# Indirect gathers issued behind other engines' steps: behind tanh in an attention, behind expert units in a tail

## The chip, the core, the metric

The kernel runs on one core of a Trainium2 chip. A time is the device time of one execution in microseconds (us); the time of the kernel is the median of ten. The engines are called PE (matrix multiply), ACT (activations), DVE (vector), POOL (GpSimd) and SP (which only issues DMAs here). Each engine works through its own list of instructions in order; engines wait for each other on semaphores.

## What is computed

The input is 4 images of 32 x 96 positions with 256 channels: 12288 tokens in 4 batches of 3072. Layer 0 is a group norm and two state space scans, along the 96 segments and along the 32 variables. Layer 1 first has an additive attention in each batch, and then a mixture of experts whose gates come from a graph attention over 1048576 edges. Only the parts named below matter here.

```python
# attention: q = t @ Wt, k = t @ Wx, t = layer norm of the tokens
h = tanh(q[:, :, None, :] + k[:, None, :, :] + bh)        # 3072 x 3072 x 32 in each batch
a = softmax(h @ Wa); t = t + a @ t_normed
# graph attention over edges src -> dst; indices past the last token are clamped or dropped
e = leaky_relu(a_src[src] + a_dst[dst])
ee = exp(e - e_max[dst]); alpha = ee / segment_sum(ee, dst)[dst]
agg = segment_sum((x @ W_gat)[src] * alpha, dst)          # 4 heads x 4 features for each token
w = softmax(top2(mean over heads(layer_norm(agg))))       # gates of 4 experts
out = sum over experts e of w_e * (gelu(x @ W1[e] + b1[e]) @ W2[e] + b2[e])
```

## The kernel before, in words

**Stages.** Layer 0 runs first, with the attention of the batches that are done beside it. The last attention, of batch 3, runs after layer 0 has ended; beside it run a sort of the edges on DVE, a count of the edges that end at the last token (class `Edges`), and expert units whose gates are not yet needed. Then comes `tail`: the rest of the expert units, the graph attention, and the sums weighted by gates. The order of instructions on PE, ACT, DVE and POOL is the order in which the program is written; no scheduler changes it, but for the few instructions after the tail.

**The last attention.** Each of its 768 slots has one tanh on ACT (`th`, L814, 128 x 3072, three buffers), 16 matmuls that read it two slots later (`pe`, L787), and small steps of softmax, transposes and products. `steps()` runs between them: in each slot it adds some DVE work of the sort, some PE work of the count (`pc`, L1216) and of early expert units. When the sort and the count are done, it makes a pool `late2` in the memory that they have left, loads the experts' weights there, and places the tile `gd` there. From then on each slot issues two indirect gathers on POOL:

```python
for _ in range(2 if columns else 0):
    ed.gather(*columns.pop(0))
```

One gather fetches, for each of 128 partitions, one row of 4 floats from the table `tab_a` into a column of `gd` (L1037); the rows' numbers are in `di`, which the sort made. There are 4 parts of 108 columns, one part for each batch of destinations. Parts 0 to 2 (324 gathers) can be fetched in the last attention; part 3 (108 gathers) needs that attention's result.

**The tail.** PE, ACT and DVE work through steps `t`. An expert unit (a block of 512 tokens and one expert) takes three steps: four times a product `ph` (L1608) with its gelu (L1690) into the tile `h1` (two buffers), and one unit later two outputs `po` (L1616) whose sum with a bias DVE writes to the tile `ko` (L1680, two buffers), from where SP stores it (`kept`). 37 units are left for the tail, which is 111 steps. Beside them 36 groups of 12 edge columns run: group `m` has its scores (L1331 to L1335, L1258, L1259) at step `G0 + PART * m // 2`, with `G0, PART = 10, 5`, and in the steps after it three spreads (DVE: one-hots `ol`, `oh` at L1350, `rh` at L1354) and three placements (PE: `pa`, L1364, 24 matmul records for a group). Each quarter of the groups closes with `finish` (L1374 to L1433), which makes the gates of six blocks. A block's final sum then reads its four stored outputs (`all`) and its tokens (`y`), 16 additions on DVE (L1693), and stores the result; these sums stand four steps apart, from the step after the gates are ready on.

**The gathers of the tail.** Group `j` needs 12 gathers from `tab_s` into `gs` (L1314, four buffers), and while part 3 of `gd` is missing each group's batch brings 4 gathers of it along: 16 for a group up to `j = 26`, 12 after that, 540 in all. The first group's gathers are issued ahead of the step loop, ahead of a POOL reduction `topa` (L1280); those of group `j` are placed ten steps ahead of its scores. On POOL nothing else stands between them; a gather waits only for the buffer that it writes and for the eighth gather before it.

Of the kernel before, what the change touches and what calls it, by code (L numbers as in the profile page):

```python
# [26 lines left out]
P = 128  # L27
# [32 lines left out]
G1, K1 = 8, 4  # L60
GP, GG = 12, 4
EDGE_US = 2.4
G0, PART = 10, 5
KO_BUFS = 2
SLOT_US, PRODUCT_US = 1.2, 0.11
EU, EG = 32, 2
# [572 lines left out]
class Attention:  # L639
# [4 lines left out]
    def __init__(self, ctx, tc, ident, a, x1, x2, xn2T, tab_s, tab_a):  # L644
        self.nc = nc = tc.nc
        self.ident, self.x1, self.x2, self.xn2T = ident, x1, x2, xn2T
        self.tab_s, self.tab_a = tab_s, tab_a
        pool = lambda name, bufs, **k: ctx.enter_context(
            tc.tile_pool(name=name, bufs=bufs, side="right", **k))
        const = self.const = pool("atc", 1)  # L650
        self.rows, self.th, self.wk = pool("atr", 2), pool("atb", TH_BUFS), pool("atw", 1)
        self.ps_e = pool("ate", PE_BUFS, space=PSUM)
        self.ps_v = pool("atv", PV_BUFS, space=PSUM)

        def load(name, shape, ap):
            t = const.tile(shape, F32, tag=name, name=name)
            nc.sync.dma_start(t, ap)
            return t

        self.wt = load("wt_rep", [P, KC, P], a["wt_rep"].rearrange("(k p) m -> p k m", p=P))  # L660
        self.wx = load("wx_rep", [P, KC, P], a["wx_rep"].rearrange("(k p) m -> p k m", p=P))
        self.bh = load("bh_rep", [P, 1], a["bh_rep"])
        self.wa = load("wa_blk", [P, P // (4 * R_ATT), QU], a["wa_blk"])
        self.ba = load("ba_rep", [P, 1], a["ba_rep"])
        self.wg = load("wg", [P, KC, HF], a["W_gat"].rearrange("(k p) f -> p k f", p=P))
        self.asr = load("as_rep", [P, HF], a["as_rep"])
        self.adr = load("ad_rep", [P, HF], a["ad_rep"])
        self.eps = const.tile([P, 1], F32, tag="eps1", name="eps1")
        nc.vector.memset(self.eps, 1e-5)

        self.sel = const.tile([P, QU], F32, tag="sel", name="sel")
        nc.vector.tensor_tensor(self.sel, ident[:, :QU], ident[:, QU:2 * QU], ALU.add)
        for q in range(2, P // QU):
            nc.vector.tensor_tensor(self.sel, self.sel, ident[:, q * QU:(q + 1) * QU], ALU.add)
        self.state = [{} for _ in range(B)]

        self.krep, self.qsel = ([const.tile([P, n], F32, tag=f"{k}{i}", name=f"{k}{i}") for i in range(2)]
                                for k, n in (("krep", TOK), ("qsel", TOK // R_ATT)))
        self.extra, self.entry, self.col, self.asked, self.normed = 0.0, 0, 0, 0, 0

        self.later = []

    def psum(self, name):
        return self.ps_v.tile([P, JB], F32, tag="pv", name=name)
# [90 lines left out]
    def units(self, side):  # L775
# [24 lines left out]
        while i < B * PER + LAG or todo or self.later:  # L800
# [10 lines left out]
            if b < B:  # L811
                s = self.state[b]
                th = self.th.tile([P, TOK], F32, tag="th", name="th")
                nc.scalar.activation(th, s["krep"], AF.Tanh, bias=s["qsel"][:, col:col + 1])  # L814
                behind.append(th)
            yield
            late, self.later = self.later, []
            for f in late:
# [192 lines left out]
class Edges:  # L1011
# [3 lines left out]

    def __init__(self, ctx, tc, a):
        self.nc, self.tc, self.a, self.todo = tc.nc, tc, a, []
        keep = ctx.enter_context(tc.tile_pool(name="el", bufs=1))  # L1020
        new = lambda name, shape, dt=F32: keep.tile(shape, dt, tag=name, name=name)
        self.cnt = new("cnt", [P, NH])
        self.lost = new("lost", [P, 1])
        self.si, self.di = new("si", [P, 4, CQ], I32), new("di", [P, 4, CQ], I32)
        self.lane, self.tile = new("lane", [P, 4, CQ]), new("tile", [P, 4, CQ])
        self.lanes, self.tiles = new("lanes", [P, P]), new("tiles", [P, NH])
        self.nc.sync.dma_start(self.lanes, a["lanes"])

    def places(self, pool, tab_a):

        self.gd = pool.tile([P, 4, CQ, HEADS], F32, tag="gd", name="gd")
        self.tab_a, self.have = tab_a, set()

    def gather(self, q, c):
        if (q, c) not in self.have:
# [57 lines left out]
    def sort(self):  # L1093
# [4 lines left out]
        with ExitStack() as ctx:  # L1098
# [73 lines left out]
            v.tensor_scalar(hi, flat(x3), 7, None, ALU.logical_shift_right)  # L1172
            v.tensor_copy(flat(self.lane), lo)
            v.tensor_copy(flat(self.tile), hi)
            yield 1.5


# [11 lines left out]
            v.tensor_copy(l4, self.lanes.unsqueeze(2).to_broadcast([P, P, K1]))  # L1189
            v.tensor_copy(t4, self.tiles.unsqueeze(2).to_broadcast([P, NH, K1]))  # L1190
            yield 1.0
            p = ctx.enter_context(tc.tile_pool(name="eo", bufs=3))
            ps = ctx.enter_context(tc.tile_pool(name="ep", bufs=1, space=PSUM))
            pc = ps.tile([P, NH], F32, tag="pc", name="pc")
            starts = [q * W2 + g for q in range(4) for g in range(0, C1, G1)]

            def one_hots(c0):
                hot = []
                for name, table, of, n in (("ol", l4, lane, P), ("oh", t4, tile, NH)):
                    t = p.tile([P, G1 // K1, n, K1], BF16, tag=name, name=name)  # L1200
                    which = of[:, c0:c0 + G1].rearrange("p (g k) -> p g k", k=K1)
                    v.tensor_tensor(t, table.unsqueeze(1).to_broadcast([P, G1 // K1, n, K1]),
                                    which.unsqueeze(2).to_broadcast([P, G1 // K1, n, K1]),
                                    ALU.is_equal)
                    hot.append(t)
                return hot

            ahead = one_hots(starts[0])
            yield G1 * (P + NH) / 1800
            for i in range(len(starts)):  # L1210
                hot, ahead = ahead, one_hots(starts[i + 1]) if i + 1 < len(starts) else None

                def products(i=i, hot=hot):
                    for u in range(G1):
                        g, k = divmod(u, K1)
                        nc.tensor.matmul(pc, hot[0][:, g, :, k], hot[1][:, g, :, k],  # L1216
                                         start=(i == 0 and u == 0),
                                         stop=(i == len(starts) - 1 and u == G1 - 1))

                self.todo.append(products)  # L1220
                yield G1 * (P + NH) / 1800
# [6 lines left out]
class Graph:  # L1228
# [4 lines left out]
    def __init__(self, ctx, tc, a, ed, tab_s, tab_a, gates):  # L1233
# [5 lines left out]
        self.bg, self.lg, self.lb = (self.load(a, k, HF) for k in ("bg_rep", "lg_rep", "lb_rep"))  # L1239
        self.eps = self.new("eps2", [P, 1])  # L1240
        self.nc.vector.memset(self.eps, 1e-5)
        self.got, self.v, self.pa = {}, {}, {}

    def new(self, name, shape):
        return self.const.tile(shape, F32, tag=name, name=name)
# [59 lines left out]
        nc.vector.tensor_tensor(wl, wl, ed.cnt.unsqueeze(2).to_broadcast([P, NH, ROW]), ALU.mult)  # L1305
        nc.vector.tensor_tensor(acc, acc, wl, ALU.add)

    def gather(self, j):
        nc, ed = self.nc, self.ed
        gs = self.wk.tile([P, GP, ROW], F32, tag="gs", name="gs", bufs=4)  # L1310
        q, c0 = divmod(j * GP, CQ)
        rows = self.tab_s.rearrange("p n f -> (p n) f")
        for u in range(GP):
            nc.gpsimd.indirect_dma_start(  # L1314
                out=gs[:, u, :], out_offset=None, in_=rows,
                in_offset=bass.IndirectOffsetOnAxis(ap=ed.si[:, q, c0 + u:c0 + u + 1], axis=0))
            ed.gather(q, c0 + u)

        for c in range(4 * j, min(4 * j + 4, CQ)):
            ed.gather(3, c)  # L1320
        self.got[j] = gs

    def scores(self, j):
        nc = self.nc
        gs = self.got.pop(j)
        q, c0 = divmod(j * GP, CQ)
        gd = self.ed.gd[:, q, c0:c0 + GP, :]
        e = self.wk.tile([P, GP, HEADS], F32, tag="e", name="e")
# [377 lines left out]
def tail(tc, a, ed, ex, w, tab_s, tab_a, gates):  # L1706


    with ExitStack() as ctx:
# [11 lines left out]
            at(2 * n, lambda: next(own, None))  # L1721
        hot, ready = {}, {}
        PQ = CQ // GP
        for m in range(4 * PQ):
            j = m
            t = G0 + PART * m // 2
            if m < 1:
                gr.gather(j)
            else:
                at(max(0, t - 10), lambda j=j: gr.gather(j))  # L1730
            at(t, lambda j=j: gr.scores(j))
            for g in range(GP // GG):
                at(t + 1 + g, lambda j=j, g=g: hot.update({(j, g): gr.spread(j, g)}))
                at(t + 2 + g, lambda j=j, g=g: gr.place(j, g, *hot.pop((j, g))))
# [36 lines left out]
        for t in range(max(3 * len(units) + 3, end)):  # L1771
# [3 lines left out]
            if n < len(units):  # L1775
# [9 lines left out]
                    ex.fetch(units[n + 1][0])  # L1785
                for f in ((0, 1), (2,), (3,))[part]:
                    ex.gelu(i, e, f, hs[n])
            if n and n - 1 < len(units) and part:
                i, e = units[n - 1]
                ex.outputs(i, e, hs[n - 1], 2 * (part - 1), to[n - 1], i not in kept)  # L1790
                if part == 2:
                    if i in kept:
                        ex.keep(i, e, to[n - 1])
# [100 lines left out]
def whole(tc, a, dram, out):  # L1894
# [11 lines left out]
    with ExitStack() as ctx:  # L1906
        actx, lctx, ectx = ExitStack(), ExitStack(), ExitStack()
        with tc.manual_schedule(engines={E.PE, E.Activation, E.DVE, E.Pool}):
# [10 lines left out]
            def steps():  # L1919
# [7 lines left out]
                lctx.close()  # L1927
                keep = ctx.enter_context(tc.tile_pool(name="late", bufs=1))
                late["gates"] = keep.tile([P, NH, NEXP], F32, tag="gates", name="gates")
                ed = late["ed"] = Edges(ctx, tc, a)  # L1930
                ex = late["ex"] = Experts(ectx, tc, x2, xn2T, late["gates"], out, dram, l0.beside)
                lists, units, columns = ed.sort(), None, []

                us_v = us_t = 0.0
                while True:
                    us_v = min(us_v, 0.0) + EDGE_US
                    while lists and us_v > 0 and len(ed.todo) < 2:
                        us = next(lists, None)
                        if us is None:
                            lists = None  # L1940
                            pool = ectx.enter_context(tc.tile_pool(name="late2", bufs=1))
                            late["w"] = Experts.weights(pool, nc, a)
                            ed.places(pool, tab_a)
                            columns = [(q, c) for q in range(B - 1) for c in range(CQ)]
                        else:
                            us_v -= us
                    yield
# [8 lines left out]
                             if (i, e) not in ex.done], a, att.krep[B % 2])  # L1956
                    while units and us_t > 0:
                        us_t -= next(units, 1.0) or 0.0
                    for _ in range(2 if columns else 0):
                        ed.gather(*columns.pop(0))  # L1960
                    yield

# [99 lines left out]
```

## Time and profile before

| what | value |
|---|---|
| median of 10 runs | 15298.12 us (15287.41 to 15314.91) |
| the profiled execution | 15310.4 us, of which the profile's span 15308.6 us |
| busy share of the span | PE 77%, ACT 80%, DVE 72%, POOL 57% |
| last attention, first tanh to last | 11773 to 14251 us |
| gathers `gd` of parts 0 to 2 | first at 13647.7 us, last at 14136.3 us |
| first product of the tail's units, first gather of the tail | 14317.0 us, 14294.2 us |
| last gather of the tail, last output of a unit | 15119.9 us, 15249.8 us |
| last addition of a final sum ends | 15303.0 us |

Read it in this way: the profile's times count from the start of its span; they are of one execution, which was 12.3 us longer than the median. A busy share is an average over stages with different limits, so what follows reads the stages by themselves: the last attention and the tail.

### The profile page before, as it was taken

What the parts mean: (1) busy time and instruction counts of PE and PEld (TensorE: products, weight loads), DVE (VectorE), ACT (ScalarE), POOL (GpSimd) and SP (SyncE); (2) the same over time, 40 slices, a digit from 0 to 9 for tenths busy, and PEclk for the clock granted to TensorE, in tenths of its full rate; (3) what the DMA queues carried; (4) which work ended last, traced back from release to release, by engine and by line L of the source; (5) the groups of instructions that cost most, each with busy time, mean ns of one, the idle gap of its engine ahead of it and who ended that gap; (6) DMA issues with size and microseconds to landing.
All of it is one profiled execution on the core that took longest, in us unless ns stands there. A gap on an engine that the chain in (4) does not pass through costs nothing. (4 is left out here: it accounts for less than half of the span.)

```text
span 15308.6 us, 224326 instructions
## 1 busy us (share of the span) xinstructions
PE 11744.2 (77%) x86496; PEld 5136.8 (34%) x86496; DVE 10995.4 (72%) x15895; ACT 12175.2 (80%) x9333; POOL 8747.2 (57%) x6402
## 2 busy tenths in 40 slices
PE   5666665777777778888887777788876778888997
PEld 2222232222222233333333333333332334433554
DVE  7888888778777887777777877577768863331367
ACT  3444434999999979999999899999997889999422
POOL 4555556777777767767777677477650000026584
PEclk8888886888888878899999889989988989999998
DMA  5666665445544444454444444355541000011235
GB/s 190 204 204 202 199 202 167 149 147 154 153 151 151 157 155 147 150 154 151 151 151 153 152 149 152 109 151 151 151 136 39 20 16 12 9 30 24 64 92 147
DMA packets 1209114, 2007.86 MB, mean 131 GB/s; under 512 B 412385, under 2 KB 655713, under 8 KB 1204961
## 3 DMA queue, kind: packets, MB, share of 16 engines
q1 hardware_dynamic: 1180384, 1988.07, 41.6%
q0 software_dynamic: 27648, 5.36, 0.9%
q8 instruction: 680, 11.14, 0.3%
q14 instruction: 402, 3.29, 0.1%
HBM read 1875.19 MB, written 117.83 MB: 130 GB/s over the span
## 5 line engine op out<-in xcount | busy, mean ns | idle before, releaser
L814 ACT ACTIVATE th<-krep,qsel 128x3072 f32<-128x3072 f32 x3072 | 8669.5, 2847 | 411.2 <-PE pe L787 393.5
L787 PE MATMUL pe<-th,wa_blk 128*32 128x384 f32 x49152 | 5058.8, 540 | 1661.6 <-ACT pr L875 1437.3
L408 POOL TENSOR_TENSOR h<-h,bC 128x768 f32<-128x768 f32 x2048 | 3753.9, 1833 | 3019.8 <-DVE h L401 2638.9
L401 DVE TENSOR_TENSOR_SCAN h<-dA,dB 128x384 f32<-128x384 f32 x4096 | 3686.1, 941 | 1037.5 <-ACT dA L384 717.4
L787 PEld LDWEIGHTS pe<-th,wa_blk 128*32 128x32 f32 x49152 | 1453.4, 116 | 4245.7 <-issue 1990.0
L392 DVE TENSOR_TENSOR dB<-bB,dtu 128x768 f32<-128x768 f32 x2048 | 1941.7, 948 | 126.5 <-DMA bB<-bc 94.0
L384 ACT ACTIVATE dA<-dt,t_A 128x380 f32<-128x380 f32 x2048 | 1126.5, 570 | 900.5 <-DVE h L401 895.9
L384 ACT ACTIVATE dA<-dt,d_A 128x372 f32<-128x372 f32 x2048 | 1102.7, 561 | 607.3 <-DVE h L401 602.7
L427 PE MATMUL py<-h,ident 128*128 128x384 f32 x2176 | 981.2, 582 | 687.9 <-POOL h L408 686.8
L415 POOL TENSOR_TENSOR h<-h 128x768 f32<-128x768 f32 x752 | 1418.9, 1887 | 53.7
L950 POOL TENSOR_SCALAR sf<-sel,f 128x32 f32<-128x32 f32 x384 | 148.8, 412 | 2252.0 <-ACT f L946 2252.0
L891 PE MATMUL pv<-xn,pT 128*32 128x257 f32 x18432 | 1113.3, 390 | 141.7 <-DVE pT L884 140.7
L884 DVE COPY pT<-ptw 128x512 f32<-128x512 f32 (+1 forms) x768 | 418.8, 545 | 713.3 <-PE ptw L882 713.1
L427 PEld LDWEIGHTS py<-h,ident 128*128 128x128 f32 x2176 | 431.4, 216 | 1246.7 <-POOL h L408 1023.6
L891 PEld LDWEIGHTS pv<-xn,pT 128*32 128x32 f32 x18432 | 582.9, 112 | 727.5 <-DVE pT L884 269.6
L417 POOL TENSOR_TENSOR y<-y,h 128x384 f32<-128x384 f32 x752 | 782.6, 1041 | 59.0
L416 POOL TENSOR_TENSOR h<-h 128x384 f32<-128x384 f32 x752 | 782.0, 1040 | 59.0
L1314 POOL DMA_INDIRECT gs<-tab_s,si x432 | 533.8, 1236 | 155.5 <-issue 147.3
L893 DVE COPY pvs<-pv 128x257 f32<-128x257 f32 x384 | 160.5, 418 | 591.6 <-PE pv L891 590.2
L882 PE MATMUL ptw<-ident,pr 128*128 128x128 f32 x2304 | 476.6, 324 | 117.0 <-DVE pT L884 46.4
L868 DVE TENSOR_REDUCE nb<-pe 128x1 f32<-128x768 f32 x384 | 361.7, 942 | 253.9 <-PE pe L787 253.8
L1037 POOL DMA_INDIRECT gd<-tab_a,di x432 | 428.9, 993 | 199.0 <-issue 130.4
(291 smaller groups left out, 14832.1 us busy)
## 6 DMA issues: line engine op xcount, KB each, us to landing
bB<-bc SPq DMA_DIRECT2D x2048, 384.0 KB
bC<-bc SPq DMA_DIRECT2D x2048, 384.0 KB
all<-kept SPq DMA_DIRECT2D x24, 2048.0 KB
x<-x SPq DMA_DIRECT2D x144, 256.0 KB
kept<-ko SPq DMA_DIRECT2D x59, 512.0 KB
x<-x SPq DMA_DIRECT2D x192, 128.0 KB
xt<-xn2T SPq DMA_DIRECT2D x41, 512.0 KB
qsel<-xn2T SPq DMA_DIRECT2D x75, 256.0 KB
```

The costliest lines, as they stand in the source:

```text
L384: nc.scalar.activation(inner(dA[:, :T]), inner(blk["dt"][:, e, :]), AF.Exp, scale=blk["w"]["A"][:, e, i + s:i + s + 1])
L392: nc.vector.tensor_tensor(dB, blk["bB"].pop(j), z["dtu"].unsqueeze(1).to_broadcast([P, SB, T]), ALU.mult)
L401: nc.vector.tensor_tensor_scan(h[:, s, :], z.pop(("dA", e, i + s))[:, :T], z["dB"][:, s, :], 0.0, ALU.mult, ALU.add)
L408: nc.gpsimd.tensor_tensor(h, h, blk["bC"].pop(j), ALU.mult)
L415: nc.gpsimd.tensor_tensor(h0, h0, h1, ALU.add)
L416: nc.gpsimd.tensor_tensor(h0[:, 0, :], h0[:, 0, :], h0[:, 1, :], ALU.add)
L417: nc.gpsimd.tensor_tensor(y[e], y[e], h0[:, 0, :], ALU.add)
L427: nc.tensor.matmul(z["py"], self.ident, h[:, s, :], start=(i == 0), stop=(i == DS - 1))
L787: nc.tensor.matmul(pe[q * QU:(q + 1) * QU, j, :KQ // 2], self.wa[:, k, :], th[:, c0:c0 + KQ // 2], start=(k == 0), stop=(k == NK - 1))
L814: nc.scalar.activation(th, s["krep"], AF.Tanh, bias=s["qsel"][:, col:col + 1])
L891: nc.tensor.matmul(pv[q * QU:(q + 1) * QU, :C + 1], pT[:, i, q * QU:(q + 1) * QU], s["xn"][:, q * NK + i, :], start=(i == 0), stop=(i == N ...
L1314: nc.gpsimd.indirect_dma_start(out=gs[:, u, :], out_offset=None, in_=rows, in_offset=bass.IndirectOffsetOnAxis(ap=ed.si[:, q, c0 + u:c0 + ...
```

## The change

- **In the last attention**: `gd` gets a place of its own (pool `late1`) before the sort begins. The gathers of parts 0 to 2 start when the lists of indices are made (`listed`), ahead of the count, and not after it. A slot issues one gather instead of two, and ahead of it a small POOL instruction, `pace` (128 x 32, an addition), that reads the slot's `th`.
- **In the tail**: the gathers are taken from a generator, `gathers()`, in the order of groups, the 4 of part 3 spread between the 12. 14 are issued ahead of the loop (`FIRST`; 16 before). Then, behind each gelu and each output of a unit, `some()` adds `RATE` = 2.75 to a credit, issues a `pace` that reads the tile just written (`h1` or `ko`), and as many gathers as the credit has. No gather of a group is issued before the scores of the group four ahead of it have been; `scores(j)` itself takes what its group still lacks.
- `PART` goes from 5 to 6: a group each three steps instead of each two and a half, so the last scores stand at step 115 instead of 97.
- The one-hots of the count are written to three tiles that the sort has left, instead of a pool with three buffers of its own.

```diff
-G0, PART = 10, 5
+FIRST, RATE = 14, 2.75
+G0, PART = 10, 6
...
                 behind.append(th)
+                self.now = th
+            else:
+                self.now = None
...
+    def behind(self, t):
+        self.nc.gpsimd.tensor_scalar(self.pace, t, 1.0, None, ALU.add)
...
             v.tensor_copy(flat(self.tile), hi)
+            self.listed = True
             yield 1.5
...
-            p = ctx.enter_context(tc.tile_pool(name="eo", bufs=3))
+            places = [lists.tile([P, W1], BF16, tag=k, name=f"hot_{k}") for k in ("move", "keep", "go")]
...
-    def gather(self, j):
+    def gathers(self):
...
+        for j in range(4 * CQ // GP):
+            while j >= self.scored + 4:
+                yield False
+            gs = self.wk.tile([P, GP, ROW], F32, tag="gs", name="gs", bufs=4)
+            q, c0 = divmod(j * GP, CQ)
+            more = list(range(4 * j, min(4 * j + 4, CQ)))
+            for u in range(GP):
+                nc.gpsimd.indirect_dma_start(
+                    out=gs[:, u, :], out_offset=None, in_=rows,
+                    in_offset=bass.IndirectOffsetOnAxis(ap=ed.si[:, q, c0 + u:c0 + u + 1], axis=0))
+                yield True
+                for which in [(q, c0 + u)] + [(3, c) for c in more[u // 3:u // 3 + 1] if u % 3 == 0]:
+                    if which not in ed.have:
+                        ed.gather(*which)
+                        yield True
+            self.got[j] = gs
...
+        def scores(j):
+            while j not in gr.got:
+                next(gathers)
+            gr.scores(j)
+
+        def some(t):
+            if credit[0] is None:
+                return
+            credit[0] += RATE
+            if credit[0] >= 1:
+                ed.behind(t)
+            while credit[0] >= 1:
+                credit[0] -= 1
+                more = next(gathers, None)
+                if more is None:
+                    credit[0] = None
+                    return
+                if not more:
+                    credit[0] = 0.0
+
+        for _ in range(FIRST):
+            next(gathers)
         for m in range(4 * PQ):
             j = m
             t = G0 + PART * m // 2
-            if m < 1:
-                gr.gather(j)
-            else:
-                at(max(0, t - 10), lambda j=j: gr.gather(j))
-            at(t, lambda j=j: gr.scores(j))
+            at(t, lambda j=j: scores(j))
...
                     ex.gelu(i, e, f, hs[n])
+                    some(hs[n][:, f, :QU])
...
                 ex.outputs(i, e, hs[n - 1], 2 * (part - 1), to[n - 1], i not in kept)
+                some(to[n - 1][:, 2 * part - 1, :QU])
...
+                ed.places(ectx.enter_context(tc.tile_pool(name="late1", bufs=1)))
...
-                            ed.places(pool, tab_a)
-                            columns = [(q, c) for q in range(B - 1) for c in range(CQ)]
...
-                    for _ in range(2 if columns else 0):
+                    if columns and ed.listed and att.normed > columns[0][0] and att.now:
+                        ed.behind(att.now[:, :QU])
                         ed.gather(*columns.pop(0))
```

More of the change, by code (lines that the diff above doesn't have):

```diff
@@ L679, in __init__ @@
         self.extra, self.entry, self.col, self.asked, self.normed = 0.0, 0, 0, 0, 0
-        self.later = []
+        self.later, self.now = [], None
     def psum(self, name):
@@ L1011, with __init__ @@
 class Edges:
-    def __init__(self, ctx, tc, a):
-        self.nc, self.tc, self.a, self.todo = tc.nc, tc, a, []
+    def __init__(self, ctx, tc, a, tab_a):
+        self.nc, self.tc, self.a, self.todo, self.tab_a = tc.nc, tc, a, [], tab_a
         keep = ctx.enter_context(tc.tile_pool(name="el", bufs=1))
@@ L1026, in __init__, with places @@
         self.lanes, self.tiles = new("lanes", [P, P]), new("tiles", [P, NH])
+        self.pace, self.listed = new("pace", [P, QU]), False
+        self.have = set()
         self.nc.sync.dma_start(self.lanes, a["lanes"])
-    def places(self, pool, tab_a):
+    def places(self, pool):
         self.gd = pool.tile([P, 4, CQ, HEADS], F32, tag="gd", name="gd")
-        self.tab_a, self.have = tab_a, set()
+    def behind(self, t):
+        self.nc.gpsimd.tensor_scalar(self.pace, t, 1.0, None, ALU.add)
     def gather(self, q, c):
@@ L1195, in sort, with one_hots @@
             starts = [q * W2 + g for q in range(4) for g in range(0, C1, G1)]
-            def one_hots(c0):
+            def one_hots(i):
                 hot = []
-                for name, table, of, n in (("ol", l4, lane, P), ("oh", t4, tile, NH)):
-                    t = p.tile([P, G1 // K1, n, K1], BF16, tag=name, name=name)
+                c0, place = starts[i], places[i % len(places)]
+                for o, table, of, n in ((0, l4, lane, P), (G1 * P, t4, tile, NH)):
+                    t = place[:, o:o + G1 * n].rearrange("p (g n k) -> p g n k", n=n, k=K1)
                     which = of[:, c0:c0 + G1].rearrange("p (g k) -> p g k", k=K1)
@@ L1206, in one_hots @@
                 return hot
-            ahead = one_hots(starts[0])
+            ahead = one_hots(0)
             yield G1 * (P + NH) / 1800
             for i in range(len(starts)):
-                hot, ahead = ahead, one_hots(starts[i + 1]) if i + 1 < len(starts) else None
+                hot, ahead = ahead, one_hots(i + 1) if i + 1 < len(starts) else None
                 def products(i=i, hot=hot):
@@ L1241, in __init__ @@
         self.nc.vector.memset(self.eps, 1e-5)
-        self.got, self.v, self.pa = {}, {}, {}
+        self.got, self.v, self.pa, self.scored = {}, {}, {}, 0
     def new(self, name, shape):
@@ L1306, in own_edges @@
         nc.vector.tensor_tensor(acc, acc, wl, ALU.add)
-    def gather(self, j):
+    def gathers(self):
         nc, ed = self.nc, self.ed
-        gs = self.wk.tile([P, GP, ROW], F32, tag="gs", name="gs", bufs=4)
-        q, c0 = divmod(j * GP, CQ)
         rows = self.tab_s.rearrange("p n f -> (p n) f")
[L1313 to L1321, printed above, removed]
+        for j in range(4 * CQ // GP):
[14 more added lines that the diff above has]
+            self.got[j] = gs
     def scores(self, j):
         nc = self.nc
-        gs = self.got.pop(j)
+        gs, self.scored = self.got.pop(j), j + 1
         q, c0 = divmod(j * GP, CQ)
@@ L1723, in tail @@
         PQ = CQ // GP
+        gathers, credit = gr.gathers(), [0.0]
+        def scores(j):
[18 more added lines that the diff above has]
+            next(gathers)
         for m in range(4 * PQ):
@@ L1929, in steps @@
                 late["gates"] = keep.tile([P, NH, NEXP], F32, tag="gates", name="gates")
-                ed = late["ed"] = Edges(ctx, tc, a)
+                ed = late["ed"] = Edges(ctx, tc, a, tab_a)
                 ex = late["ex"] = Experts(ectx, tc, x2, xn2T, late["gates"], out, dram, l0.beside)
-                lists, units, columns = ed.sort(), None, []
+                ed.places(ectx.enter_context(tc.tile_pool(name="late1", bufs=1)))
+                lists, units = ed.sort(), None
+                columns = [(q, c) for q in range(B - 1) for c in range(CQ)]
                 us_v = us_t = 0.0
```

## The prediction

> **What bounds the kernel now.** I read the page's slices first, for the stages, then a table of windows over the tail, the waits in it, and the timelines of POOL, DVE and PE there. The edit touches only the last quarter of the span.
>
> ```profile
> ACT  3444434999999979999999899999997889999422
> POOL 4555556777777767767777677477650000026584
> ```
>
> A digit is the busy share of 383 us. The last attention (11773 to 14251 us, slices 31 to 38) is ACT's: in 13000 to 13500 us, the windows show ACT busy for 483.49 of 500 us. POOL is idle there until the burst of gathers from 13647 us on, and in the window 13660 to 14160, under that burst, ACT is as full: 480.84 of 500. So those 324 gathers cost nothing now; the list of line 1037 there also shows nobody who waited for them. What can be won lies in the tail:
>
> ```profile
> core 0: us, PE busy (x) PEld busy (x) DVE busy (x) ACT busy (x) POOL busy (x), PEclk, DMA share, GB/s
> 14322.00:14576.00 254.00, 251.96 (x777) 147.27 (x776) 135.78 (x203) 65.52 (x84) 202.93 (x169) 1.00 0.28 69
> 14576.00:14956.00 380.00, 342.96 (x992) 192.39 (x992) 260.11 (x476) 85.32 (x107) 303.83 (x249) 0.96 0.39 96
> 14956.00:15121.00 165.00, 154.42 (x458) 87.81 (x457) 127.69 (x244) 44.27 (x54) 131.92 (x109) 0.97 0.48 122
> ```
>
> PE is full at first and loses 37 us in the middle window. POOL's 80% there is no slack: the missing fifth is the gap of 0.30 us behind each gather. The waits, in us, times, longest, say who is late:
>
> ```profile
> PE pa L1364 <- DVE rh L1354: 44.3, 13, 11.1
> DVE e L1331 <- DMA gs<-tab_s,si: 43.3, 11, 8.8
> ```
>
> PE waits for DVE's spreads as long as DVE waits for gathers: POOL sets the pace from about group 9 to group 27. Its timeline, and DVE's beside it, show what a gather costs:
>
> ```profile
> 14604.53 0.94 POOL L1314 DMA_INDIRECT gs<-tab_s,si  x1 [0.30 <-issue]
> 14605.77 1.84 POOL L1314 DMA_INDIRECT gs<-tab_s,si  x1 [0.30 <-issue]
> 14607.92 2.93 POOL L1037 DMA_INDIRECT gd<-tab_a,di  x1 [0.31 <-issue]
> ...
> 14604.64 2.16 DVE L1354 TENSOR_TENSOR rh<-oh,v 128x1920 f32<-128x1920 f32 x1
> 14607.87 2.16 DVE L1354 TENSOR_TENSOR rh<-oh,v 128x1920 f32<-128x1920 f32 x1
> ```
>
> Alone a gather takes 0.94 + 0.30 us. One that meets `rh` ends 0.81 us (14607.61 against 14606.80) or 0.82 us (14610.85 against 14610.03) after it, so `rh` holds it up. With that, the 416 gathers of groups 1 to 26 took 14322.3 to 14956.1, which is 1.524 us each and 24.4 for a group of 16. PE's price for the same is read from the starts of its rows:
>
> ```profile
> 15099.34 3.60 PE L1608 MATMUL ph<-xt,w 128*128 128x512 f32 x8
> 15102.77 3.38 PE L1364 MATMUL pa<-rh,ol 128*128 128x480 f32 x8
> 15105.99 1.88 PE L1608 MATMUL ph<-xt,w 128*128 128x512 f32 x4
> 15107.71 3.62 PE L1616 MATMUL po<-w,h 128*128 128x256 f32 x16
> 15111.16 3.38 PE L1364 MATMUL pa<-rh,ol 128*128 128x480 f32 x8
> ```
>
> 8 `ph` take 3.43 us, 8 `pa` 3.22, 16 `po` 3.45. A unit (16 `ph`, 32 `po`) is 13.77 us, a group (24 `pa`) 9.66. At two and a half steps a group, PE needs 13.77 x 2.5 / 3 + 9.66 = 21.1 us while POOL needs 24.4: that is the starvation. All 37 units and 36 groups are 857 us; 14317 to 15247 are 930, less 51 of waits 879, so 2.6% more than the sum, which I keep as a factor.
>
> **The last attention.** 324 gathers move forward, to slots 2494 to 2818 of the 3072 tanhs (12487 to 13465 us), each with a `pace`. In a slot of 3.01 us (166 tanhs in 500 us) POOL has 1.25 + 0.36 us of work, and behind it are only the four `sf` of a tile. The new wait is ACT's: a tanh must also wait for POOL's read of the buffer of three slots before. The read comes at most a stretched gather after its tanh, and there are two slots, 6 us, of cover: 0. If that cover went, ACT would pay, as the bound. The earlier place of `gd` takes away a wait of 58.5 us that POOL had for the count, which nobody waited for: 0. DVE's, PE's and ACT's orders in this stage stay as they are, the moved one-hot tiles are three as before: 0.
>
> **POOL in the tail.** No gather is removed: still 540. Added are 209 paces, 156 of them ahead of gather 431 of 540, the last of group 26. The nearest row is `sf`, of the same form:
>
> ```profile
> L950 POOL TENSOR_SCALAR sf<-sel,f x28: 352/355/367, 13680.3 to 14271.9; 128x32 f32<-128x32 f32 x28
> ```
>
> It takes 0.355 us. The gap from `sf` to a gather is 0.16 us (row at 13877.71), and the 0.30 between two gathers is replaced. If nothing stands between gather and pace, a pace adds 0.355 + 0.16 - 0.30 = 0.22 us; with a whole gap of 0.30, 0.52. I take 0.40: part of the gap is the gather's own, and each pace has two semaphores to check. A unit then costs POOL 24.4 + 6 x 0.40 = 26.8 us, and PE (13.77 + 9.66) x 1.026 = 24.0 at `PART` 6. So POOL stays the bound, and its shortfall of 3.3 us a group becomes 2.8.
>
> **The new wait, and who is behind it.** Before, POOL's lateness reached PE through missing data, which now comes with three groups to spare. Now the reads are what counts: the first gelu of unit n+2 writes the `h1` that POOL reads in unit n, and `ko` of unit n+1 the one it reads in unit n. A gelu that waits for POOL stops ACT's scores' exponentials behind it, its banks of `ph`, and so PE; a `ko` that waits stops DVE's spreads. ACT and DVE can be some four steps ahead of POOL, no more, already from unit 6 or 7 on, since the units ahead of the first group need 13.8 us of PE and 23 of POOL.
>
> **The sum, on the profiled execution.** POOL starts at 14322; gathers 15 to 431 take 417 x 1.524 = 635.5, paces 156 x 0.40 = 62: gather 431 is issued at 15020. It stands at step 79, so ACT is at about 83. From there to the last output, in step 113, PE has 9 units of `ph` (62), 10 of `po` (69) and 30 sets of `pa` (97), 228 x 1.026 = 233, and POOL, with 12 gathers a group (18.3 us before, now 20.7), is no longer the bound: the last `ko` is at 15253. Before it was here:
>
> ```profile
> 15249.09 0.68 DVE L1680 TENSOR_TENSOR ko<-po,b 128x512 f32<-128x512 f32 x1
> ...
> 15295.04 7.92 DVE L1693 SCALAR_TENSOR_TENSOR y<-all,gates,y 128x256 f32<-128x256 f32 x16 [2.03 <-DMA y<-x]
> ```
>
> Then comes what `PART` 6 does to the end. Before, the last `finish` (15197 to 15222) lay beside units; from the last `ko` to the end were 59.5 us, of six block sums at 9.6, whose inputs' transfers set their pace. Now the scores of group 35 stand at step 115, behind the last unit. After the last `ko`, DVE has in its order five spreads (3.1 each, 15.5), a score (3.1), three halves of block sums (6), a wait for the last placement (1.3), about 2 of waiting at `n`, which needs the last store of `ko` and now stands in the last score (at most 3: before, it ran 9.7 us after that `ko`, and here DVE is there after 6.6), and a `finish` (24.8): 53. Only then follow the six blocks, 57.8 as in 15245.2 to 15303.0, and 5.6 to the span's end. Sum 15253 + 53 + 57.8 + 5.6 = 15369, against 15308.6: 61 us longer. The median lies 10.5 us under that span; 15298 + 61 gives 15359.
>
> **A rule beside this.** The Trainium skill ("SBUF — State Buffer", section "Who interferes with whom") says that a VectorE instruction with two SBUF inputs contends with a GpSimd instruction that reads SBUF, and that whichever comes second blocks fully. That speaks against the paces, which read SBUF: the rows above show it for `rh`, none shows it for a small POOL read or for the short `ol` and `y`. By the rule a pace that arrives at random waits 0.28 us for `rh` (108 x 2.158² / 2 over 900 us) and 0.07 for the others, which is 156 x 0.35 = 55 us more, 15414; by the row alone `rh` is already in the 1.524, and the sum stays 15359.
>
> **Rivals.** *POOL stops being the bound.* If gathers that start behind a gelu miss `rh`, POOL's unit falls from 26.8 to 16 x 1.245 + 2.4 = 22.3 us, and anything under PE's 24.0 decides for it. Then PE alone sets 14317 + (37 x 13.77 + 34.7 x 9.66) x 1.026 + 7 of its waits for `ko` = 15190, and the longer end adds 116.4: 15307, no change; 15296 in the median, 15268 if PE also ran at the full clock without those waits. For it: 4.4 us of the 24.4 are hold-ups by `rh`. Against: a POOL that is late is never idle, and meets each of the 108 `rh`. *Paces are dear.* Each waits for DVE's short instructions as well, or the wait on two semaphores shows: with a whole gap (0.52) and the mean hold-up of a gather (4.4 / 16 = 0.28) a pace adds 0.80 us instead of 0.40, 62 more, 15421. For it: how `rh` holds a gather; against: gathers over `ol` or `y` are hardly longer. *The last attention pays.* ACT waits for POOL in slots where one-hots (0.69 + 0.55 us, one pair in 5 us) hold gathers up: at 0.1 us a slot 32 us, 15391. Against: two slots of cover. That the change doesn't do what it says is excluded by the built order, which has the paces and waits as told.
>
> **How the numbers follow.** A measurement can tell some 0.2%, 30 us, from no change: 15267 to 15329 is "same". Forecast, POOL bound through its own reads: 0.65, own range 15331 (0.22 a pace) to 15378 (0.52). POOL not the bound: 0.22, 15268 to 15296, of which I give 0.07 to an end still shorter than counted, below 15267. Dear paces 0.09, attention 0.04. Slower 0.73, same 0.20, faster 0.07. The range takes in the upper half of the second case and reaches halfway to the dear paces: 15288 to 15400.
>
> **What would show it.** Right: POOL without idle time from 14322 to about 15020; gelus of the tail waiting for POOL where none do now; `e` hardly waiting for gathers; tanh at 2845 ns and ACT full in the last attention; the last `finish` after the last `ko`, some 110 us ahead of the end. Wrong: paces that wait for gelus throughout (then POOL has slack, and the first rival holds), paces over 0.6 us, gathers of the tail at 0.95 us in the mean, or a last tanh that has moved from 14251.

## The result and the profile after

The changed kernel takes 15352.5 us (median of 8 runs, 15341.4 to 15369.9) where the kernel before took 15298.1: a ratio of 1.0036, with a 95% interval of 1.0027 to 1.0045. The profiled execution of the changed kernel has a span of 15333.5 us and took 15335.4, which is 17.1 below the median, where that of before was 12.3 above it; so stages are compared, not spans.

From the first product of the tail's units to the end of the span it is 1050.5 us (14283.0 to 15333.5), where it was 991.6: 58.9 more. The last attention, from first tanh to last, is 2464.0 us (2477.5). The first tanh is 20.5 us earlier, but that point lies between 11747 and 11781 us in the profiles of this study, in kernels that are all alike up to there.

The windows over the tail of the changed kernel, with the columns of the table before:

```profile
core 0: us, PE busy (x) PEld busy (x) DVE busy (x) ACT busy (x) POOL busy (x), PEclk, DMA share, GB/s
14322.00:14576.00 254.00, 230.89 (x690) 132.52 (x689) 107.55 (x161) 53.38 (x70) 212.72 (x215) 0.98 0.20 43
14576.00:14956.00 380.00, 346.44 (x1017) 199.33 (x1016) 253.94 (x470) 84.82 (x108) 320.41 (x313) 0.95 0.36 96
14956.00:15121.00 165.00, 152.72 (x449) 87.26 (x448) 116.39 (x219) 39.79 (x50) 139.30 (x139) 0.97 0.37 105
```

POOL is as full as a row of gathers with gaps can be, and PE loses 23 us in the first window already, where it lost 2 before. The waits of the tail (total, times, longest) name the new chain:

```profile
ACT h L1709 <- POOL pace L1042: 477.2, 26, 23.8
DVE v L1271 <- ACT v L1270: 235.2, 36, 14.2
PE pa L1383 <- DVE rh L1373: 39.0, 9, 8.6
PE po L1635 <- DVE ko L1699: 28.6, 13, 5.1
```

None of these gelus (`h`) waited for POOL before. Behind a gelu that waits stands ACT's exponential of the scores (L1270), behind that DVE's `v` and spread, and behind that PE, which waits for `rh` about as long as before (44.3) and for `ko` longer (6.8 before). DVE's `e`, which waited 43.3 us for gathers before, waits for none. The timeline of DVE shows the end:

```profile
15224.85 0.68 DVE L1699 TENSOR_TENSOR ko<-po,b 128x512 f32<-128x512 f32 x1
...
15253.88 0.65 DVE L1393 TENSOR_TENSOR acc<-acc,pa 128x480 f32<-128x480 f32 x1
...
15320.21 7.92 DVE L1712 SCALAR_TENSOR_TENSOR y<-all,gates,y 128x256 f32<-128x256 f32 x16 [0.49 <-DMA y<-x]
```

The last `finish` begins with `acc` 29 us after the last `ko`; the six block sums come behind it. From the last `ko` to the end are 108.6 us (59.5 before), and from the first product to the last `ko` 941.9 (932.1): of the 58.9 us, 49.1 lie behind the last `ko` and 9.8 ahead of it.

### The profile page after: what moved, and what is told of

The parts are those of the page before. It is cut to its first block, busy times and chain, and to the rows that moved or that the text cites. A ratio compares the mean times of both kernels' runs of the same rounds, so it can differ in the third digit from the quotient of the medians.

```text
span 15333.5 us, 225352 instructions
## 1 busy us (share of the span) xinstructions
PE 11744.8 (77%) x86496; PEld 5152.4 (34%) x86496; DVE 10998.9 (72%) x15895; ACT 12161.9 (79%) x9327; POOL 8983.3 (59%) x6935
## 4 chain that ended last, share of the span: by engine, by line
ACT 17%; PE 15%; DVE 9%; issue 4%; POOL 4%; DMA 1%; SPq 0%; POOLq 0%; DVEq 0%; ACTq 0%
ACT th L815 12%; PE pe L788 7%; PE pv L895 2%; ACT dA L385 2%; POOL gs L1332 2%; DVE h L402 1%; ACT pr L879 1%; PE po L1635 1%; DVE go L1085 1%; PE ptw L886 1%; PE ph L1627 1%; POOL gd L1047 1%; PE pa L1383 1%; PE ex L1552 0%; PE pc L1228 0%
## 5 line engine op out<-in xcount | busy, mean ns | idle before, releaser
L815 ACT ACTIVATE th<-krep,qsel 128x3072 f32<-128x3072 f32 x3072 | 8668.0, 2847 | 388.2 <-PE pe L788 370.8
L1709 ACT ACTIVATE h<-ph,b 128x512 f32<-128x512 f32 x148 | 96.5, 685 | 662.9 <-POOL pace L1042 477.2
L886 PE MATMUL ptw<-ident,pr 128*128 128x128 f32 x2304 | 479.3, 326 | 113.1 <-DVE pT L888 43.3
L1047 POOL DMA_INDIRECT gd<-tab_a,di x432 | 469.4, 1087 | 142.6 <-issue 135.4
```

## The experiments

My theory after the result: that split is also the split of causes, 49 us from `PART` 6 and its longer end, the rest from gelus and `ko` that wait for POOL's reads. The rivals: all of it is the paces', or all of it `PART`'s; and of the paces, their waits or their work.

**Parts alone.** No paces in the tail, and beside it `PART` 6 alone in the kernel before:

```diff
 e1, in some():
-            if credit[0] >= 1:
-                ed.behind(t)
 e4, in the kernel before:
-G0, PART = 10, 5
+G0, PART = 10, 6
```

> The changed kernel without the 209 paces of the tail; the order of the gathers among the groups, PART 6 and the attention's part stay. Theory (half of the price is the longer end from PART 6, the rest is POOL's own reads of h1 and ko, which hold up ACT and DVE): nothing couples ACT to POOL any more, a unit costs POOL 16 x 1.524 = 24.4 us against PE's 24.0, the wait of gelus for paces (477 us in the changed kernel) is gone; first product to last ko falls from 941.9 us to about 895, the end stays 109 us; about 15306, 45 us under the changed kernel. Rival 'only PART': paces cost nothing, the time stays at 15352 within 8 us. Rival 'all from the paces': the end becomes short too, and the time falls under 15280.

> The kernel before with G0, PART = 10, 6 alone: no pace anywhere, gathers ten steps ahead as before. Theory: PE needs 24.0 us a unit and POOL 24.4, so the starvation of the tail (44 us of PE waiting for spreads) is mostly gone, and the end after the last ko grows from 59.5 to about 110: 15295 to 15305, no change. Rival 'the whole price is PART 6': 15350.

Measured: 15284.5 us without paces (0.9990 of before, 0.9981 to 0.9999), 15298.1 with `PART` 6 alone (0.9998, 0.9989 to 1.0007). In e1 the last `ko` comes 874.0 us after the first product and the end takes 109.0 us; in e4 it is 877.3 and 108.8. So `PART` 6 costs 49 us at the end and gives back 55 ahead of it (932.1 to 877.3). The windows from the first product to the last `ko`, of before, e4, e1 and the changed kernel, show where the 55 come from (columns as in the table of windows above):

```profile
14317.00:15249.09 932.09, 878.83 (x2641) 506.05 (x2639) 619.68 (x1112) 224.11 (x282) 638.97 (x525) 0.98 0.38 99
14297.90:15175.10 877.20, 853.80 (x2601) 496.91 (x2599) 569.97 (x1004) 214.95 (x271) 656.41 (x525) 0.99 0.40 97
14294.10:15168.09 873.99, 851.51 (x2601) 496.46 (x2599) 570.17 (x1005) 215.03 (x271) 657.36 (x527) 0.99 0.39 98
14283.00:15224.85 941.85, 872.24 (x2601) 503.97 (x2599) 571.24 (x1004) 210.39 (x271) 740.33 (x736) 0.97 0.34 91
```

PE stands idle for 53 us before and 23 in e4: 30 of the 55 are starvation that is gone. The other 25 are in PE's busy time. Of these, some 16 are the 40 `pa` that now come behind the last `ko` (five spreads at 3.22 us), so that much is moved and not saved. In the changed kernel PE is idle for 70 us, in e1 for 22. `PART` 6 is free by itself, and the 68 us between e1 and the changed kernel are the paces'. My split of causes was wrong: the end is longer in all three, but the paces bring back the idle time that `PART` 6 takes away.

**The paces: waits or work.** First a pace that waits for nobody and that nobody waits for:

```diff
-                ed.behind(t)
+                ed.behind(ed.lanes[:, :QU])
```

> The changed kernel with the 209 paces of the tail reading a constant tile of the same size instead of h1 or ko: POOL's instructions are the same in number and form, but they wait for no gelu, and no gelu or ko waits for them. If the price of the paces is the wait of gelus for POOL's reads (theory): first product to last ko about 905 us instead of 942, time about 15315. If it is POOL's added work that counts (late gathers again): DVE's scores wait for gathers as before the change, and the time stays at 15352 within 10 us.

Measured: 15336.6 us (1.0023, 1.0012 to 1.0034), 16 less than the changed kernel, not 37. The waits of gelus for paces are gone, and POOL's lateness comes through the data again:

```profile
DVE e L1350 <- DMA gs<-tab_s,si: 139.5, 17, 14.2
```

Gather 431 is done 714.6 us after the first product (e1: 650.8), so 156 paces cost 0.41 us each with no wait for ACT or DVE's tiles in them. Work, then, is worth 52 us in e2, and the coupling through `h1` and `ko` is left with 16 of the 68. That is the least it can be, if the two add up: in the changed kernel gather 431 is done earlier, after 699.8 us, so its paces cost POOL (699.8 - 650.8) / 156 = 0.31 us each against e1, and less of its 68 us is work. If it is work, twice the paces cost twice as much:

```diff
                 ed.behind(t)
+                ed.behind(t)
```

> The changed kernel with each pace of the tail issued twice, one straight behind the other. Theory (a pace's own work on POOL is the price, and POOL is the bound through gather 431): 156 more paces at 0.40 us, 62 us more, 15415; at 0.22 us, where the second is rarely held up, 34 more, 15386. Rival (what costs is that POOL's order is tied to ACT's steps, not the work): the second pace finds its tile written and adds nothing, 15352 within 8 us.

Measured: 15413.8 us (1.0081, 1.0067 to 1.0094), 61.3 over the changed kernel; gather 431 is done 764.3 us after the first product, where it was 699.8: 64.5 / 156 = 0.41 again. And with `PART` 5, where the end is short:

```diff
-FIRST, RATE = 14, 2.75
-G0, PART = 10, 6
+FIRST, RATE = 14, 3.3
+G0, PART = 10, 5
```

> The changed kernel with PART 5, as before the change, and RATE 3.3, so that the gathers keep up with the faster groups (one pace for 3.3 gathers, 126 of them ahead of gather 431 instead of 156). Theory (POOL's added work is the price, whatever PART is): 417 gathers as before 637.9 us, 126 paces at 0.40 us 50 more, then 294 to the last ko as before and an end of 59.5: 1042 us from the first product, 15344. Rival (the price is the longer end that PART 6 brings): 49 us less than the changed kernel, 15303.

Measured: 15350.9 us (1.0044, 1.0030 to 1.0058). The end is 60.7 us, 48 less than in the changed kernel, and the last `ko` comes after 1004.2, 62 later: the stretch ahead loses what the end gains. 133 paces stand ahead of gather 431 (not 126), which is done after 692.7 us; in e3 below, with `PART` 5 and no paces in the tail, after 640.5: 52.2 / 133 = 0.39. The price is there with `PART` 5 too, and the rival at 15303 falls.

**What of a pace costs.** Instead of an addition that reads, a fill of the same tile:

```diff
-                ed.behind(t)
+                tc.nc.gpsimd.memset(ed.pace, 0.0)
```

> The changed kernel with the 209 paces of the tail replaced by fills of the same tile with zeros: POOL's instructions are as many, but they read no memory and wait for no other engine, and nothing waits for them. Beside the run whose paces read a constant (15336.6 us, paces 0.567 us in the mean, held by rh to 0.157 us after its end). If it is POOL's read that the spreads hold up, as the Trainium skill's rule on two-input vector operations has it: the fill takes about 0.32 us in the mean, 46 us of hold-ups go, and the time is about 15300. If any POOL instruction is held: 15337 within 10 us.

Measured: 15279.4 us (0.9993, 0.9984 to 1.0002), with 209 more instructions on POOL than e1 and no time for them. The 15300 expected had a fill at 0.32 us; it takes 0.142. The groups of POOL in the tail, of e2 and then of e9:

```profile
L1042 POOL TENSOR_SCALAR pace<-lanes 128x32 f32<-128x32 f32 x209 | 118.5, 567 | 16.5 <-issue 11.4
```

```profile
L1756 POOL MEMSET pace<- 128x32 f32 x209 | 29.8, 142 | 0.5
```

The timelines of e2 and of e9, POOL's rows and the `rh` beside them, show the rest:

```profile
14818.64 2.20 DVE L1373 TENSOR_TENSOR rh<-oh,v 128x1920 f32<-128x1920 f32 x1
...
14819.62 1.37 POOL L1042 TENSOR_SCALAR pace<-lanes 128x32 f32<-128x32 f32 x1
14821.16 1.19 POOL L1332 DMA_INDIRECT gs<-tab_s,si  x1 [0.17 <-issue]
```

```profile
14525.92 2.16 DVE L1373 TENSOR_TENSOR rh<-oh,v 128x1920 f32<-128x1920 f32 x1
...
14526.74 0.15 POOL L1756 MEMSET pace<- 128x32 f32 x1
14527.06 1.84 POOL L1332 DMA_INDIRECT gs<-tab_s,si  x1 [0.17 <-issue]
```

A pace that reads is held until 0.15 us after `rh` (14820.99 against 14820.84); a fill passes in 0.15 us with `rh` running, and only the gather behind it is held, to 0.82 us after it. Unheld, a fill takes 0.142 us in the gap that two gathers leave anyway: 0.142 + 0.17 - 0.30 = 0.01. An addition takes 0.315 + 0.02 + 0.17 - 0.30, and the gather behind it 1.03 us instead of 0.945: 0.29 together. Held up, e2's 209 additions lose 53 us (0.567 against 0.315), but the gathers lose less in exchange: their mean falls from 1.241 (e1) to 1.200 us though 201 of them are 0.085 longer, 39 us in all. So most of the 0.41 is the addition's own 0.29; the hold-ups leave (53 - 39) / 209 = 0.07, and the rest is not accounted for. The fill differs from it in operation as well as in reading, so the runs do not part those two.

**The attention alone,** in front of the tail of before (`PART` 5, no paces in the tail, gathers placed ten steps ahead):

```diff
         for m in range(4 * PQ):
...
-            at(t, lambda j=j: scores(j))
+            if m < 1:
+                gr.gather(j)
+            else:
+                at(max(0, t - 10), lambda j=j: gr.gather(j))
+            at(t, lambda j=j: gr.scores(j))
```

> The kernel before with the attention's part of the change alone: the 324 gathers one per slot behind the slot's tanh, gd and the one-hots at their new places; the tail as before. Theory: 15298 within 5 us; tanh of the last attention 2845 ns, first tanh to last 2477 us. Rival 'the attention gains what the changed profile showed' (2464.0 us from first tanh to last, 13.4 less): 15285. Rival 'ACT pays for POOL's reads': 15330.

Measured: 15289.7 us (0.9992, 0.9983 to 1.0001), 2467.3 us from first tanh to last. ACT's waits from 12500 to 14235 us, of e4, whose attention is that of before, and of e3:

```profile
ACT th L814 <- PE pe L787: 58.9, 95, 2.1
```

```profile
ACT th L814 <- PE pe L787: 51.2, 76, 2.1
```

The tanhs wait 7.7 us less for PE, and that is most of the 10. The time alone is not clear of noise, but the stage is: it takes 2460.7 to 2470.8 us in all eleven profiles with the paced gathers, 2477.5 and 2477.6 in the two with those of before. Most of it is not the burst of gathers that is spared: 7.3 of the 10.2 us lie in slots 288 to 575, and the first gather of before comes in slot 576. Why PE is earlier there is not settled.

**A version to beat both.** POOL is the bound as long as a group has 16 gathers, so the groups go slower up to there and faster after it (e11 and e12 with other rates):

```diff
 e10, e3 with:
-            t = G0 + PART * m // 2
+            t = G0 + (28 * m // 10 if m < 27 else 73 + 19 * (m - 26) // 10)
 e11:
+            t = G0 + (53 * m // 20 if m < 27 else 69 + 23 * (m - 26) // 10)
 e12:
+            t = G0 + (11 * m // 4 if m < 27 else 71 + 22 * (m - 26) // 10)
```

> No paces; the attention's part of the change, the gathers ten steps ahead as before, and groups at two rates in place of PART: 2.8 steps a group through group 26, while POOL has 16 gathers a group, then 1.9 steps, so that the last scores stand at step 100. Theory (before, PE starves while POOL is the bound, and PART 6 pays the gain back with a longer end): PE has 23.1 us of work a group against POOL's 24.4 and starves little, then 18.9 against 18.3; last ko some 880 us after the first product (932 before), end 60 to 65: 15298 - 10 for the attention - 45 = about 15243. Rival (the groups after 26 come too late or too dense, and DVE becomes the bound): 15285.

Measured: 15280.3 us (0.9994, 0.9985 to 1.0003), not 15243. The last `ko` comes after 910.2 us, not 880, and the end takes 70.8. PE stands idle for 38 us up to the last `ko`; its timeline shows one place, with 10 of them, the third `finish` (14971.8 to 15023.4), which now meets spreads that stand close:

```profile
14980.39 8.40 PE L1375 MATMUL pa<-rh,ol 128*128 128x480 f32 x16 [4.04 <-DVE rh L1365]
...
15008.49 8.31 PE L1375 MATMUL pa<-rh,ol 128*128 128x480 f32 x16 [6.14 <-DVE rh L1365]
```

The rates of e11 and e12 were to mend that:

> As the kernel with two rates, but 2.65 steps a group through group 26 and 2.3 after it (last scores at step 99). In the run with 2.8 and 1.9 PE lost some 30 us where the third finish met spreads that stood too close, and the end after the last ko was 71 us. Theory: PE starves for some 10 us before group 26, little after it, the end is 60 to 65: first product to last ko 900, 15265 in the median. Rival (every schedule of the groups pays for POOL's 417 gathers in some place): 15280, as with the other kernels without paces.

> The same with 2.75 steps a group through group 26 and 2.2 after it (last scores at step 100). Theory: first product to last ko 895, end 65, 15265. Rival: 15280.

Measured: 15362.3 and 15336.2 us, but beside them the kernel before took 15736.5 us, 438 more than at first (0.9763, 0.9749 to 0.9778, and 0.9746, 0.9732 to 0.9760). They say nothing on the rates, but something else, with the two runs that follow. The third run beside them left out the paces of e3's attention:

```diff
-                        ed.behind(att.now[:, :QU])
```

> The attention's part of the change without its 324 paces (gathers one per slot from the sort's end on, in POOL's own order, tied to no tanh); the tail as before. The attention's part with paces measured 15289.65 us and 2467 us from the first tanh to the last, against 2477.5 before. If the 10 us come from the gathers' earlier place: 2467 us again, 15290. If the paces bring them, by keeping gathers away from other work: 2477 us, 15299.

Measured: 15693.5 us (0.9977, 0.9967 to 0.9988). Its attention takes 2808.7 us, 341 more than with paces, all of it while the gathers run (12471.6 to 13715.9): 96 slots take 397, 393 and 389 us there, in e12 with paces 290, 289 and 283. PE's timeline, and POOL's beside it:

```profile
12667.21 0.80 PE L787 MATMUL pe<-th,wa_blk 128*32 128x384 f32 x1 [0.60 <-issue]
12669.30 0.80 PE L787 MATMUL pe<-th,wa_blk 128*32 128x384 f32 x1 [1.30 <-issue]
12671.40 0.80 PE L787 MATMUL pe<-th,wa_blk 128*32 128x384 f32 x1 [1.30 <-issue]
...
12669.90 0.95 POOL L1046 DMA_INDIRECT gd<-tab_a,di  x1 [0.30 <-issue]
12671.16 0.95 POOL L1046 DMA_INDIRECT gd<-tab_a,di  x1 [0.30 <-issue]
```

The gathers follow each other at their usual 0.95 + 0.30 us, while PE's matmuls, 16 in 1.50 us a little earlier, come one by one, 0.7 to 2.8 us apart, waiting for nothing that the profile shows. The 324 gathers come in eleven runs of at most 32, some 40 us long; spread over them, the 341 us are an estimated 31 for a run. The granted clock reads 0.80 from 12600 to 12700 us, where it is 0.95 in e3. That is too little for gaps of 2 us between matmuls of 0.8; whether it is a cause or a result is not shown. The last run asked whether a few paces in the tail are enough there, and how their price goes:

```diff
             credit[0] += RATE
-            if credit[0] >= 1:
-                ed.behind(t)
+            if credit[0] < 3 * RATE:
+                return
+            ed.behind(t)
```

> The changed kernel with a pace at every third step of the tail only, and up to eight gathers behind it (70 paces instead of 209, about 52 of them ahead of gather 431). Theory: a pace that reads costs POOL 0.41 us, so gather 431 comes 104 x 0.41 = 43 us earlier than in the changed kernel: 15305 to 15312, where the kernel before takes 15298. If a few paces already make POOL's reads the bound: 15335 or more. On the chip of the last three runs, where the kernel before took 15736 us and PE, ACT and DVE stood still beside runs of 33 to 49 gathers: runs of gathers are at most eight here, so nothing stands still, neither in the attention nor in the tail, and the time is 15305 to 15320 there too, 2.7% less than the kernel before.

Measured: 15331.0 us beside 15732.2 of before (0.9745, 0.9727 to 0.9763). The attention runs as in e12 (2465.9 us), but "nothing stands still" fails:

```profile
14350.32 5.71 PE L1635 MATMUL po<-w,h 128*128 128x256 f32 x16 [20.69 <-issue]
```

PE stands for 20.7 us beside runs of eight gathers with paces between them that find their tile long written, so POOL never rests. The price of 70 paces can't be read from a run with that in it.

## Why the prediction was right, point by point

- **The time.** 15359 forecast, 15352.5 measured, 54 over before; the longer tail 61 forecast, 58.9 in the profile. Several steps of the sum missed in ways that cancel, so part of the closeness is luck.
- **POOL in the tail.** 0.40 us a pace was taken, between 0.22 and 0.52. From the first product to gather 431 it is 637.9 us before and 699.8 after: 61.9 / 156 = 0.40; doubling gave 0.41. But 12.9 of the 61.9 us come without paces too (650.8 in e1, where `rh` holds gathers up more: 1.239 us in the mean up to gather 431, against 1.209 before), which leaves 0.31 for a pace; that the term came out whole is luck. (The last gather of group 26 is 432, one behind 431; nothing hangs on it.) The parts differ as well: the additions are shorter when unheld than `sf` (0.315, not 0.355), the gather behind each is 0.085 longer, and `rh` holds 27 of the 209 up, which then take 1.84 us in the mean.
- **The new wait.** It came as described, through `h1` above all; its share by e2 is 16 us or more. POOL has nothing but its gaps of 0.30 us between 14322 and 15020, as the list of signs had it.
- **The end.** 116.4 us forecast, 108.6 measured. Up to the last `finish` the 28 us came out (29.0), but by other terms: the three halves of block sums take 11.7 us and not 6, the score 1.9 and not 3.1, and the two waits counted with 3.3 do not come. The last `finish` takes 20.0 instead of 24.8 us, since one half of a block sum instead of two falls into it and no `ko`, and the six blocks 54.1 instead of 57.8. The stretch ahead of it was 5.9 us too short in the sum (936 against 941.9), so the two misses nearly cancel.
- **The last attention.** The step "0" failed: e3 is 10 us faster than before. The cost side of it held: the tanhs stayed at 2847 ns, and the rival at 15391 fell. What it left out is a gain, and the last tanh moved from 14251 to 14216.6 us, a sign that was listed as wrong (20.5 us of it are the earlier start).
- **POOL stops being the bound.** This rival's time, 15296 in the median, is what comes without paces: 15298 (e4) and 15284 (e1), with 877 and 874 us to the last `ko` where its sum had 873 (15190 less 14317). Its condition did not hold: gathers of the tail took 1.187 us, not 0.945.
- **Dear paces, and the rule.** The Trainium skill ("SBUF — State Buffer", section "Who interferes with whom") says that a VectorE instruction with two SBUF inputs contends with a GpSimd instruction that reads SBUF, and not with one that only writes. Both halves agree with the timelines above, the addition held to 0.15 us behind `rh`, the fill not, as far as these two stand for reading and not reading. As a term of the sum it would have been too much all the same (15414), because a hold-up that a pace takes is one that a gather is spared: 53 against 39 us in e2.

The reading that fell was one of afterwards, that the longer end was the price. The longer end buys off 30 us of PE's starvation and takes over work, an even trade; but with POOL at 24.4 us a group and PE at 24.0 there was no room for six additions of 0.4 us.

## What to carry to other kernels

Where an engine is the bound, a pacing instruction costs what it adds to that engine's row, whether or not anyone waits for it: about 0.3 us for an addition here, next to nothing for a fill. Test it with one that waits for nobody. A longer end and a starved middle can pay for each other, so a schedule's parts are to be run alone before the profile's split is taken for the causes. And what a pace is worth may show only in conditions that the first comparison does not have.

## What the runs showed of the hardware that was not expected

- The same kernel before took 15294 to 15300 us in three comparisons and 15732 to 15737 in the last two; the last of these was on the chip with the number of the first four experiments, so the chip alone does not explain it. In the first of those two, gathers that follow each other without rest go with single matmuls up to 2.8 us apart, and the unpaced attention takes 341 us more. One gather behind each tanh costs nothing in these two (2464 to 2467 us for the attention, 2467 in e3), and the kernels with that part of the change (e11, e12, e14) were 2.4 to 2.6% faster than the kernel before. The changed kernel itself was not run there. What differs between the two conditions, and what PE waits for, stays open.
- A POOL fill between two indirect gathers is free (0.01 us), since they leave a gap of 0.30 us that it mostly fills; an addition of the same size costs 0.29 us before any hold-up, 0.085 of it in the gather that follows.
